# Delta rule on one core: where the first substitution and the projections of the later tiles stand in a hand-written order

## Chip, core and metric

The kernel runs on one core of one Trainium2 chip. The metric is the device time of one execution in microseconds (us). Five engines work side by side and meet through semaphores: PE (matrix multiply), ACT (activation), DVE (vector), POOL (GpSimd) and SP, which here only issues DMA transfers. PEld in the profile is PE's loading of weights.

## The reference, cut to what matters

The network has eight layers over an input of 4 sequences of 1024 tokens with 128 features, each layer of the form `x = x + layer(layernorm(x))`. The change lies in the first, the delta rule, with 8 heads of 16 features:

```python
q = (x @ Wq).reshape(Bb, Ll, H, HD)
k = (x @ Wk).reshape(Bb, Ll, H, HD)
k = k / jnp.maximum(jnp.linalg.norm(k, axis=-1, keepdims=True), 1e-12)
v = jax.nn.silu(x @ Wv).reshape(Bb, Ll, H, HD)
beta = jax.nn.sigmoid(x @ Wb)
...
def step(S, inp):
    qt, kt, vt, bt = inp
    Sk = jnp.einsum('bhk,bhkv->bhv', kt, S)
    S = S + jnp.einsum('bh,bhk,bhv->bhkv', bt, kt, vt - Sk)
    ot = jnp.einsum('bhk,bhkv->bhv', qt, S)
    return (S, ot)
...
return (o - mu) / jnp.sqrt(var + 1e-05) * ln_w + ln_b
```

The seven layers behind it (feed-forward layers, attention, mixtures of experts) are the same in both kernels, and each needs the complete output of the layer ahead of it.

## The kernel before

`l0_attn` (L143) doesn't go token by token. It cuts every sequence into 32 chunks of 32 tokens (C = 32, NS = 32); one chunk of all four sequences fills the 128 partitions. Within a chunk the rule is a triangular system: the Gram matrix of the chunk's keys, scaled by beta, gives a lower triangle L, whose inverse T replaces 32 steps. Between chunks only the 16 x 16 states S are handed on.

**Two sizes of work.** A *tile* is 128 tokens of each sequence, that is four chunks; there are eight. `bring(i)` (L246) normalizes tile i on DVE (xn, four instructions), transposes it on PE (tq) and copies it on ACT into xnT. `gate(i)` (L262) computes beta: matmuls pb, tanh on ACT, one DVE instruction; for some tiles a tiny Silu (hint) goes first, so that ACT loads the table there. `expand(i, j)` (L274) projects half a tile, two chunks, to keys and values: matmuls pp, three ACT instructions (v, vk, sq), a DVE reduction of the squares (rn, L291) and a POOL product. `length(i, n)` (L297) turns rn of n tiles into the inverse norms: a square root on ACT, two DVE instructions.

**For each chunk:** `flip(c)` (L355) scales the keys on POOL, transposes them on PE (tp) and copies them on ACT (kt, bt). `gram(c)` (L372) makes the Gram matrix on PE (wide), copies it on ACT (kk, a ring of two) and sends it in four small transfers to DRAM (ld); after every fourth chunk one transfer brings four matrices back as L, now with one system per partition. `solve(n, part)` (L384) inverts the 128 systems of four chunks on DVE, column by column, 31 columns of two instructions each (L393, L396), cut into eight parts by `PARTS` (L154); after the last part T goes to DRAM (td), and `fetch(c)` (L400) brings it back a chunk at a time as tb. `apply(c)` (L417) multiplies it with keys and values (wp, wu). `attend(c)` (L437) makes the query scores on PE, and DVE masks them (mt, L440). `query(n, g)` (L406) projects the queries (pq). The recurrence itself is up, ux, sp, S, oT, ot, op, o, from L495 on.

**Order.** The scheduler is off in this stage (`manual_schedule`); every engine gets its instructions in the order in which the loop of L490 writes them. It runs over slots -12 to 34. Slot c holds the recurrence of chunk c, `gram(c + 11)`, `fetch(c + 2)`, `apply(c + 1)`, `attend(c + 2)` and `flip(c + 12)`, and one quarter of a substitution: system n is solved in slots 4n - 6 to 4n - 3, two parts a slot, one ahead of the chunk's output (L527) and one at the slot's end, behind the jobs (L556). The jobs of a slot, which are the work on tiles, stand in a table, `jobs` (L305). System 0 needs the Gram matrices of chunks 0 to 3, the last of which is made in slot -8; it is solved in slots -6 to -3. Tiles 4 to 7 are worked on in slots -8 to 0.

**Buffers.** PSUM pools: psc, one buffer (wide); psm, two buffers with tag sm (tq, pb, pp, up, wp, oT, op); ptp, one buffer with tag tp (tp, pq, and pp of tile 7); psp, one buffer for the sum that holds S.

Of the kernel before, what the change touches and what calls it, by code (L numbers as in the profile page):

```python
# [9 lines left out]
F32 = mybir.dt.float32  # L10
# [5 lines left out]
P = 128  # L16
NB, SEQ, D = 4, 1024, 128
TPB = SEQ // P
# [9 lines left out]
class Net:  # L28
# [114 lines left out]
    def l0_attn(self):  # L143
# [8 lines left out]
        H, HD, C = 8, 16, 32  # L152
# [4 lines left out]
        with ExitStack() as c_:  # L157
# [73 lines left out]
            m0 = one.tile([P, TPB, NB, 2], F32, tag="m0", name="m0")  # L231
            r0 = one.tile([P, TPB, NB], F32, tag="r0", name="r0")

            def moments_of(i):

                for b in range(NB):
                    st = two.tile([P, 6], F32, tag="st", name="st", bufs=4)
                    nc.vector.bn_stats(st, x4[:, i, b, :])
                    nc.vector.bn_aggr(m0[:, i, b, :], st)
# [6 lines left out]
            def bring(i):  # L246

                xn = two.tile([P, NB, D], F32, tag="xn", name="xn")
                tp = psm.tile([P, NB, P], F32, tag="sm", name="tq")
                for b in range(NB):  # L250
                    nc.vector.tensor_scalar(
                        xn[:, b, :], x4[:, i, b, :], m0[:, i, b, 0:1], r0[:, i, b : b + 1], ALU.subtract, ALU.mult
                    )
                    nc.tensor.transpose(tp[:, b, :], xn[:, b, :], self.ident)
                nc.scalar.copy(
                    tok[:, 4 * i : 4 * i + 4].rearrange("p c (b t) -> p b c t", b=NB),
                    tp.rearrange("p b (c t) -> p b c t", c=4),
                )
# [3 lines left out]
            def gate(i):  # L262


                if i in (0, 1, 2, 4):
                    nc.scalar.activation(hint, self.eps, AF.Silu)
                pb = psm.tile([P, 4, H], F32, tag="sm", name="pb")
                for j in range(4):
                    mm(pb[:, j, :], lhsT=tok[:, 4 * i + j], rhs=wkvb[:, 256:264], start=True, stop=True)
                bs = beta[:, 4 * i : 4 * i + 4, :]  # L270
                nc.scalar.activation(bs, pb, AF.Tanh, scale=0.5)
                nc.vector.tensor_scalar(bs, bs, 0.5, 0.5, ALU.mult, ALU.add)

            def expand(i, j):  # L274

                c2 = slice(4 * i + 2 * j, 4 * i + 2 * j + 2)
                sh = [P, 2, H, HD]
                pool, tag = (ptp, "tp") if i == TPB - 1 else (psm, "sm")
                pp = pool.tile([P, 2, 256], F32, tag=tag, name="pp")
                for a in range(2):  # L280
                    mm(pp[:, a, :], lhsT=tok[:, 4 * i + 2 * j + a], rhs=wkvb[:, 0:256], start=True, stop=True)
                v = two.tile([P, 2, D], F32, tag="v", name="v")
                nc.scalar.activation(v, pp[:, :, 128:256], AF.Silu)
                pk = pp[:, :, 0:128].rearrange("p c (h d) -> p c h d", h=H)
                nc.scalar.copy(vk[:, c2, :, 0:HD], pk)
                sq = two.tile(sh, F32, tag="sq", name="sq")
                if i == 1:
                    nc.gpsimd.tensor_mul(sq, vk[:, c2, :, 0:HD], vk[:, c2, :, 0:HD])
                else:
                    nc.scalar.square(sq, pk)  # L290
                nc.vector.tensor_reduce(rn[:, c2, :], sq, axis=AX.X, op=ALU.add)  # L291
                nc.gpsimd.tensor_mul(
                    vk[:, c2, :, HD:], v.rearrange("p c (h d) -> p c h d", h=H),
                    beta[:, c2, :].unsqueeze(3).to_broadcast(sh),
                )

            def length(i, n):  # L297
# [9 lines left out]
                -11: [(gate, 1), (expand, 1, 0), (moments_of, 6), (moments_of, 7), (begin, 0)],  # L307
                -10: [(expand, 1, 1), (begin, 1)],
                -9: [(length, 1, 1), (roots_of, 4, 4), (masks,)],
                -8: [(bring, 3), (bring, 4), (gate, 2), (expand, 2, 0), (zeros, 0)],  # L310
                -7: [(expand, 2, 1), (bring, 5), (gate, 3), (expand, 3, 0), (zeros, 1)],
                -6: [(expand, 3, 1), (length, 2, 2), (bring, 6), (zeros, 2)],
                -5: [(bring, 7), (gate, 4), (expand, 4, 0), (zeros, 3)],
                -4: [(expand, 4, 1), (gate, 5), (expand, 5, 0)],
                -3: [(expand, 5, 1), (gate, 6), (expand, 6, 0)],
                -2: [(expand, 6, 1), (gate, 7)],
                -1: [(expand, 7, 0)],
                0: [(expand, 7, 1), (length, 4, 4)],
            }
            moments_of(0)  # L320
            roots_of(0, 1)
# [33 lines left out]
            def flip(c):  # L355

                kn = kns[c % len(kns)]
                nc.gpsimd.tensor_mul(kn[:, :, 0:HD], vk[:, c, :, 0:HD], spread(rn[:, c, :]))
                nc.gpsimd.tensor_mul(vk[:, c, :, 0:HD], kn[:, :, 0:HD], spread(beta[:, c, :]))
                tp = ptp.tile([P, 2, 2, P], F32, tag="tp", name="tp")  # L360
                for i, t in enumerate((kn, vk[:, c])):
                    for g in range(2):
                        nc.tensor.transpose(
                            tp[:, i, g, :], t[:, 4 * g : 4 * g + 4, :].rearrange("p a b -> p (a b)"), self.ident
                        )
                kt = two.tile([P, 2, P], F32, tag="kt", name="kt", bufs=LAG + 3)
                nc.scalar.copy(kt, tp[:, 0])
                bt = two.tile([P, 2, P], F32, tag="bt", name="bt", bufs=3)
                nc.scalar.copy(bt, tp[:, 1])
                kT[c] = (kt, bt)  # L370
# [35 lines left out]
            def query(n, g):  # L406

                if g == 0:
                    qs[n] = two.tile([P, 4, 2, P], F32, tag="qp", name="qp")
                pq = ptp.tile([P, 2, 2, P], F32, tag="tp", name="pq").rearrange("p a b c -> p (a b c)")  # L410
                mm(
                    pq, lhsT=wqp[:, 4 * g : 4 * g + 4, :].rearrange("p a b -> p (a b)"),
                    rhs=tok[:, 4 * n : 4 * n + 4], start=True, stop=True,
                )
                nc.scalar.copy(qs[n][:, :, g, :], pq.rearrange("p (c t) -> p c t", c=4))

            def apply(c):  # L417

                tb = tbs[c % len(tbs)]
                wp = psm.tile([P, 2, P], F32, tag="sm", name="wp")  # L420
                for g in range(2):
                    for j in range(4):
                        mm(
                            wp[32 * j : 32 * j + 32, g, :], lhsT=vk[:, c, 4 * g + j, :], rhs=tb[:, 2 * j + g, :],
                            start=True, stop=True,
                        )
                wu = two.tile([P, 2, P], F32, tag="wu", name="wu")
                nc.scalar.copy(wu, wp)
                return wu
# [60 lines left out]
            for slot in range(-LAG - 1, NS + 3):  # L490
                c, part = slot, (slot + 6) % 4
                n = (slot + 6) // 4
                cut = (2 * part, 2 * part + 1) if 0 <= n < NS // 4 else ()
                if 0 <= c < NS:
                    mt = late.pop(c)  # L495
                    up = psm.tile([P, 2, 64], F32, tag="sm", name="up")
# [30 lines left out]
                for i in cut[0:1]:  # L527
                    solve(n, i)
                if 0 <= c < NS:
                    oT = psm.tile([P, 2, P], F32, tag="sm", name="oT")  # L530
                    for g in range(2):
                        for j in range(4):
                            mm(
                                oT[32 * j : 32 * j + 32, g, :], lhsT=u[:, 4 * g + j, :], rhs=mt[:, 2 * j + g, :],
                                start=True, stop=True,
                            )
                    ot = two.tile([P, 2, P], F32, tag="ot", name="ot")
                    nc.scalar.copy(ot, oT)
                if 0 <= c + 2 < NS:
                    late[c + 2] = attend(c + 2)  # L540
                if 0 <= c < NS:
                    op = psm.tile([P, 2, 64], F32, tag="sm", name="op")
# [10 lines left out]
                    flip(c + LAG + 1)  # L553
                for job, *args in jobs.get(slot, ()):
                    job(*args)
                for i in cut[1:]:  # L556
                    solve(n, i)
                if slot in reloads:
# [1177 lines left out]
```

## Time and profile before

| what | value |
|---|---|
| three timed runs | 2819.35, 2822.51, 2824.38 us (median 2822.51) |
| the profiled execution | 2822.76 us |
| its span, first to last instruction | 2821.0 us |
| delta-rule stage, start to last copy of o (L550) | 0 to 370.2 us |
| DVE busy in the span | 1829.0 us (65%) |
| PE busy in the span | 2554.4 us (91%) |
| start of the mask multiply mt (L440) in slots -2, 0, 2, 4, 8, 12 | 103.5, 116.9, 139.2, 154.6, 186.2, 216.1 us |

Times in the profile count from the start of the span. A row of the timeline gives start, duration, engine, line, operation, what is written and read, and in square brackets how long the engine was idle ahead of it and what ended that idle time. A chain of waits is given by the page too, but its detail begins only after the delta-rule stage; there the stage has to be read from the timeline and the table of stages. PE works each float32 matmul in two passes, so eight matmuls appear as 16.

### The profile page before, as it was taken

How to read it: one execution, taken by the hardware profiler on the slowest of the kernel's cores; microseconds unless marked ns; L12 is line 12 of the kernel's file. 1: busy time of each engine (PE TensorE's matmuls, PEld its weight loads, DVE VectorE, ACT ScalarE, POOL GpSimd, SP SyncE). 2: the span in 40 equal slices, each digit the busy share in tenths (PEclk: the TensorE clock that was granted, in tenths of full speed). 3: DMA queues.
4: the chain of work that ended last, by engine and by line, in shares of the span. 5: the costliest groups of instructions: out<-in, count | busy, mean ns of one | idle time of the engine just before them, and what ended most of it. 6: DMA issues, size and time to landing. Idle time of an engine off the chain costs nothing.

```text
span 2821.0 us, 51973 instructions
## 1 busy us (share of the span) xinstructions
PE 2554.4 (91%) x20384; PEld 1288.8 (46%) x20384; DVE 1829.0 (65%) x3838; ACT 1549.5 (55%) x3520; POOL 172.1 (6%) x286
## 2 busy tenths in 40 slices
PE   5687768999998959999999768999999999999967
PEld 4455536699985533333333343333333333333356
DVE  4788867566663666677676146767776777777234
ACT  4565466655553450665666660666666666666642
POOL 3212000000000000000000050000000000000001
PEclk7899869899998975999999865999999999999968
DMA  2233320000000000010110000000000000000000
GB/s 54 57 74 70 74 64 1 1 2 2 1 2 1 1 1 16 10 16 13 16 18 10 5 1 8 8 8 11 9 9 9 8 12 8 10 8 8 3 9 24
DMA packets 116485, 46.62 MB, mean 17 GB/s; under 512 B 88419, under 2 KB 110860, under 8 KB 116237
## 3 DMA queue, kind: packets, MB, share of 16 engines
q1 hardware_dynamic: 116236, 43.25, 7.7%
q8 instruction: 163, 2.67, 0.4%
q14 instruction: 86, 0.70, 0.1%
HBM read 16.95 MB, written 12.98 MB: 11 GB/s over the span
## 4 chain that ended last, share of the span: by engine, by line
PE 63%; DVE 3%; ACT 2%; POOL 1%; issue 1%; DMA 0%; SPq 0%; POOLq 0%; DVEq 0%; ACTq 0%
PE pb L1261 30%; PE po L1283 15%; PE pa L1236 6%; PE ep L1053 2%; PE tp L119 2%; PE pp L1176 1%; PE gp L1001 1%; PE bp L1066 1%; DVE st L81 1%; ACT xn L108 1%; PE pv L1157 1%; PE op L695 1%; PE bp L1064 0%; DVE mv L82 0%; PE op L694 0%
## 5 line engine op out<-in xcount | busy, mean ns | idle before, releaser
L1265 ACT ACTIVATE es<-pb 128x512 f32<-128x512 f32 x1536 | 836.0, 594 | 561.5 <-PE pb L1261 406.8
L1261 PE MATMUL pb<-q,k 32*128 32x512 f32 x3072 | 957.7, 642 | 0.7 <-ACT es L1265 0.7
L1236 PE MATMUL pa<-k,q 32*128 32x512 f32 x3072 | 912.8, 680 | 16.9 <-DMA q<-q 16.0
L1248 DVE TENSOR_REDUCE bm<-pa 128x2 f32<-128x1024 f32 x512 | 625.9, 1225 | 275.6 <-PE pb L1261 169.7
L1283 PE MATMUL po<-es,v 128*32 128x256 f32 (+1 forms) x5760 | 480.0, 405 | 0.0
L1261 PEld LDWEIGHTS pb<-q,k 32*128 32x128 f32 x3072 | 314.9, 184 | 347.4 <-ACT es L1265 188.9
L1244 DVE TENSOR_REDUCE bm<-pa 128x16 f32<-128x1024 f32 x256 | 312.6, 1222 | 107.4 <-PE pb L1261 60.7
L1283 PEld LDWEIGHTS po<-es,v 128*32 128x32 f32 x5760 | 114.2, 108 | 543.1 <-issue 510.5
L1236 PEld LDWEIGHTS pa<-k,q 32*128 32x128 f32 x3072 | 253.6, 193 | 94.3 <-DVE bm L1248 50.5
L119 PE MATMUL tp<-ident,xn 128*128 128x128 f32 x192 | 65.5, 440 | 56.9 <-ACT xn L108 51.0
L1290 DVE COPY oT<-po 128x512 f32<-128x512 f32 x48 | 32.7, 682 | 109.1 <-PE po L1283 109.1
L393 DVE TENSOR_TENSOR pr<-T,L 128x31 f32<-128x31 f32 (+15 forms) x248 | 95.3, 384 | 7.1
L396 DVE TENSOR_TENSOR T<-T,pr 128x31 f32<-128x31 f32 (+15 forms) x248 | 91.3, 368 | 8.5
L108 ACT ACTIVATE xn<-x,nm,rs 128x128 f32<-128x128 f32 x224 | 89.3, 481 | 7.7 <-DVE nm L105 7.7
L119 PEld LDWEIGHTS tp<-ident,xn 128*128 128x128 f32 x192 | 34.4, 186 | 88.4 <-ACT xn L108 73.2
L1062 DVE SCALAR_TENSOR_TENSOR x<-ep,g,x 128x128 f32<-128x128 f32 x160 | 55.0, 349 | 29.7 <-ACT sc L1060 20.0
L807 ACT ACTIVATE w<-tr,half 128x128 f32<-128x128 f32 x128 | 47.0, 367 | 48.0 <-PE tr L805 45.1
L782 ACT ACTIVATE a<-hp,wb 128x128 f32<-128x128 f32 x128 | 47.1, 368 | 40.8 <-PE hp L778 39.8
L1053 PE MATMUL ep<-L_ffn_expert_w,xnT 128*128 128x512 f32 x128 | 67.9, 620 | 0.0
L513 PE MATMUL sp<-ux,kn 128*128 128x256 f32 x128 | 48.2, 512 | 20.1 <-ACT ux L502 20.1
L1535 POOL MEMSET c<- 128x512 f32 (+1 forms) x2 | 2.3, 1164 | 1021.9 <-PE tp L119 1021.9
L81 DVE BATCH_NORM_STATS2 st<-x 128x6 f32<-128x128 f32 x224 | 57.2, 265 | 9.6 <-PE op L545 4.0
(451 smaller groups left out, 3572.3 us busy)
## 6 DMA issues: line engine op xcount, KB each, us to landing
ld<-kk SPq DMA_DIRECT2D x128, 32.0 KB
L<-ld SPq DMA_DIRECT2D x8, 512.0 KB
td<-T SPq DMA_DIRECT2D x8, 512.0 KB
tb<-td SPq DMA_DIRECT2D x128, 32.0 KB
md<-nt SPq DMA_DIRECT2D x192, 2.0 KB
q<-md SPq DMA_DIRECT2D x192, 2.0 KB
od<-o SPq DMA_DIRECT2D x32, 64.0 KB
on<-od SPq DMA_DIRECT2D x8, 256.0 KB
```

The source lines that it names most:

```text
L81: nc.vector.bn_stats(st, src[:, i, :])
L108: nc.scalar.activation(dst[:, i, :], src[:, i, :], AF.Identity, bias=nm[:, i : i + 1], scale=rs[:, i : i + 1])
L119: nc.tensor.transpose(tp[:, i, :], xn[:, 4 * q + i, :], self.ident)
L393: nc.vector.tensor_mul(pv, T[:, 0 : j + 1, j : j + 1].to_broadcast(sh), L[:, j : j + 1, j + 1 :].to_broadcast(sh))
L396: nc.vector.tensor_sub(T[:, 0 : j + 1, j + 1 :], T[:, 0 : j + 1, j + 1 :], pv)
L1053: nc.tensor.matmul(ep.rearrange("p a b -> p (a b)"), lhsT=self.tok(t), rhs=ew[:, 4 * h : 4 * h + 4, :].rearrange("p a b -> p (a b)"), star ...
L1236: nc.tensor.matmul(pa[:, j % 2, :], lhsT=st["q"][r, i * P : (i + 1) * P], rhs=st["k"][r, n * 512 : (n + 1) * 512], start=True, stop=True,)
L1244: nc.vector.tensor_reduce(out[:, :, 1:9], pa.rearrange("p j (c s) -> p j c s", c=8), axis=AX.X, op=ALU.max)
L1248: nc.vector.tensor_reduce(out[:, :, n : n + 1], pa, axis=AX.X, op=ALU.max)
L1261: nc.tensor.matmul(pb, lhsT=st["k"][r, kc * P : (kc + 1) * P], rhs=st["q"][r, n * 512 : (n + 1) * 512], start=True, stop=True,)
L1265: nc.scalar.activation(es[turn][:, j, :], pb, AF.Exp, scale=scale)
L1283: nc.tensor.matmul(po[r, cols], lhsT=vring[b % 2][:, kc, 4 * g + j, :], rhs=es[:, j, cols], start=kc == 0, stop=True, skip_group_check=True,)
```

## The change

Three things change, all in `l0_attn`.

1. Substitution 0 is taken out of slots -6 to -3 (`0 < n` in `cut`) and put at the end of the jobs of slots -8 (parts 0 and 1), -7 (parts 2 to 4) and -6 (parts 5 to 7). Substitution 1 and the others stay in their slots.
2. Tiles 4 to 7 are worked on later and a piece at a time: tile 4 in slots -5 to -2, tile 5 in slots -3 to 0, tile 6 in slots 4 to 7, tile 7 in slots 8 to 10. `length`, formerly once for tiles 4 to 7, comes in two calls, in slots 1 and 11. The table hint comes for tile 6 as well.
3. Projections of tiles 5 to 7 (tq, pb, pp) take their PSUM buffer from ptp, those of tiles 0 to 4 from psm (`bank`). Tags are renamed to ps in both pools.

```diff
+            def bank(i):
+                return ptp if i > 4 else psm
...
-                tp = psm.tile([P, NB, P], F32, tag="sm", name="tq")
+                tp = bank(i).tile([P, NB, P], F32, tag="ps", name="tq")
...
-                if i in (0, 1, 2, 4):
+                if i in (0, 1, 2, 4, 6):
                     nc.scalar.activation(hint, self.eps, AF.Silu)
-                pb = psm.tile([P, 4, H], F32, tag="sm", name="pb")
+                pb = bank(i).tile([P, 4, H], F32, tag="ps", name="pb")
...
-                pool, tag = (ptp, "tp") if i == TPB - 1 else (psm, "sm")
-                pp = pool.tile([P, 2, 256], F32, tag=tag, name="pp")
+                pp = bank(i).tile([P, 2, 256], F32, tag="ps", name="pp")
...
-                -8: [(bring, 3), (bring, 4), (gate, 2), (expand, 2, 0), (zeros, 0)],
-                -7: [(expand, 2, 1), (bring, 5), (gate, 3), (expand, 3, 0), (zeros, 1)],
-                -6: [(expand, 3, 1), (length, 2, 2), (bring, 6), (zeros, 2)],
-                -5: [(bring, 7), (gate, 4), (expand, 4, 0), (zeros, 3)],
-                -4: [(expand, 4, 1), (gate, 5), (expand, 5, 0)],
-                -3: [(expand, 5, 1), (gate, 6), (expand, 6, 0)],
-                -2: [(expand, 6, 1), (gate, 7)],
-                -1: [(expand, 7, 0)],
-                0: [(expand, 7, 1), (length, 4, 4)],
+                -8: [(bring, 3), (gate, 2), (expand, 2, 0), (zeros, 0)],
+                -7: [(expand, 2, 1), (gate, 3), (expand, 3, 0), (zeros, 1)],
+                -6: [(expand, 3, 1), (length, 2, 2), (zeros, 2)],
+                -5: [(bring, 4), (zeros, 3)],
+                -4: [(gate, 4)],
+                -3: [(expand, 4, 0), (bring, 5)],
+                -2: [(expand, 4, 1)],
+                -1: [(gate, 5), (expand, 5, 0)],
+                0: [(expand, 5, 1)],
+                1: [(length, 4, 2)],
+                4: [(bring, 6)],
+                5: [(gate, 6)],
+                6: [(expand, 6, 0)],
+                7: [(expand, 6, 1)],
+                8: [(bring, 7)],
+                9: [(gate, 7), (expand, 7, 0)],
+                10: [(expand, 7, 1)],
+                11: [(length, 6, 2)],
...
-                cut = (2 * part, 2 * part + 1) if 0 <= n < NS // 4 else ()
+                cut = (2 * part, 2 * part + 1) if 0 < n < NS // 4 else ()
...
                 for job, *args in jobs.get(slot, ()):
                     job(*args)
+                for i in {-8: (0, 1), -7: (2, 3, 4), -6: (5, 6, 7)}.get(slot, ()):
+                    solve(0, i)
                 for i in cut[1:]:
                     solve(n, i)
```

More of the change, by code (lines that the diff above doesn't have):

```diff
@@ L359, in flip @@
                 nc.gpsimd.tensor_mul(vk[:, c, :, 0:HD], kn[:, :, 0:HD], spread(beta[:, c, :]))
-                tp = ptp.tile([P, 2, 2, P], F32, tag="tp", name="tp")
+                tp = ptp.tile([P, 2, 2, P], F32, tag="ps", name="tp")
                 for i, t in enumerate((kn, vk[:, c])):
@@ L409, in query @@
                     qs[n] = two.tile([P, 4, 2, P], F32, tag="qp", name="qp")
-                pq = ptp.tile([P, 2, 2, P], F32, tag="tp", name="pq").rearrange("p a b c -> p (a b c)")
+                pq = ptp.tile([P, 2, 2, P], F32, tag="ps", name="pq").rearrange("p a b c -> p (a b c)")
                 mm(
@@ L419, in apply @@
                 tb = tbs[c % len(tbs)]
-                wp = psm.tile([P, 2, P], F32, tag="sm", name="wp")
+                wp = psm.tile([P, 2, P], F32, tag="ps", name="wp")
                 for g in range(2):
@@ L492, in l0_attn @@
                 n = (slot + 6) // 4
-                cut = (2 * part, 2 * part + 1) if 0 <= n < NS // 4 else ()
+                cut = (2 * part, 2 * part + 1) if 0 < n < NS // 4 else ()
                 if 0 <= c < NS:
                     mt = late.pop(c)
-                    up = psm.tile([P, 2, 64], F32, tag="sm", name="up")
+                    up = psm.tile([P, 2, 64], F32, tag="ps", name="up")
                     for g in range(2):
@@ L529, in l0_attn @@
                 if 0 <= c < NS:
-                    oT = psm.tile([P, 2, P], F32, tag="sm", name="oT")
+                    oT = psm.tile([P, 2, P], F32, tag="ps", name="oT")
                     for g in range(2):
@@ L541, in l0_attn @@
                 if 0 <= c < NS:
-                    op = psm.tile([P, 2, 64], F32, tag="sm", name="op")
+                    op = psm.tile([P, 2, 64], F32, tag="ps", name="op")
                     for g in range(2):
```

## Prediction

> **What bounds the kernel now.** I read the page first: the span is 2821.0 us in a profiled execution of 2822.76 us (median of the three timed runs 2822.51). Everything from about 376 us on (attention, feed-forward layers) is untouched by the change, and each later layer needs the output of the delta rule, so what the delta-rule stage gains or loses goes straight to the end. Then the table of stages (busy time of each engine in chosen stretches):
>
> ```profile
> 40.00:61.00 21.00, 16.26 (x80) 12.38 (x80) 5.46 (x20) 10.01 (x25) 4.57 (x9) 0.50 0.15 38
> 61.00:99.00 38.00, 24.82 (x172) 18.03 (x172) 28.35 (x81) 20.10 (x48) 11.44 (x21) 0.87 0.13 29
> 139.00:264.00 125.00, 103.65 (x1744) 73.36 (x1744) 108.34 (x266) 81.07 (x249) 17.49 (x34) 0.93 0.35 78
> ```
>
> The columns are us, then PE, PEld, DVE, ACT and POOL busy. From 40 to 61 us DVE works 5.5 of 21 us; between 139 and 264 us (slots 2 to 17) it works 108 of 125 us, more than ACT's 81. There DVE is the engine that sets the pace, with PE waiting for it in turn. The timeline shows when the first substitution (solve 0, L393/L396) runs, and what follows it on DVE:
>
> ```profile
> 44.39 0.34 SPq L382 DMA_DIRECT2D L<-ld  x1
> ...
> 60.67 0.42 DVE L291 TENSOR_REDUCE rn<-sq 128x16 f32<-128x256 f32 x1 [2.52 <-ACT sq L290]
> ...
> 61.01 0.18 DVE L393 TENSOR_TENSOR pr<-T,L 128x31 f32<-128x31 f32 x1
> ...
> 99.04 0.21 DVE L396 TENSOR_TENSOR T<-T,pr 128x31 f32<-128x31 f32 x1
> 99.16 0.38 DVE L393 TENSOR_TENSOR pr<-T,L 128x31 f32<-128x31 f32 x1
> 99.33 0.34 SPq L398 DMA_DIRECT2D td<-T  x1
> ```
>
> Its input was asked for at 44.39, but it starts at 61.01, ends at 99.25, and solve 1 follows with no gap. Third, the same timeline at slot 0, the one slot in full swing that in the old kernel still has projection work (expand 7,1 and length):
>
> ```profile
> 116.90 1.23 DVE L440 TENSOR_TENSOR mt<-wide,upper 128x1024 f32<-128x1024 f32 x1 [0.81 <-PE wide L352]
> ...
> 118.73 0.38 ACT L369 COPY bt<-tp 128x256 f32<-128x256 f32 x1
> ...
> 119.17 1.13 PE L281 MATMUL pp<-wkvb,xnT 128*128 128x256 f32 x4 [0.74 <-ACT bt L369]
> ...
> 120.92 0.40 ACT L290 ACTIVATE sq<-pp 128x256 f32<-128x256 f32 x1
> ...
> 121.36 0.42 DVE L291 TENSOR_REDUCE rn<-sq 128x16 f32<-128x256 f32 x1 [3.24 <-ACT sq L290]
> ...
> 122.98 0.39 DVE L300 TENSOR_SCALAR rn<-rn 128x128 f32<-128x128 f32 x1 [1.20 <-ACT rn L299]
> ```
>
> DVE stands idle for 3.24 us until ACT has squared what PE projected, which waited for the single ptp buffer until bt was copied; then 1.20 us for the square root. The substitution's second piece stands behind these on DVE. From this mask multiply (mt, L440, one a slot) to the next are 13.2 us; in slots 8, 12 and 16, which do the same pieces without jobs, 7.1, 7.8 and 8.5.
>
> **What the skill says.** "PSUM — Partial Sum Buffer", Engine vs sequencer instructions: the queues of ScalarE, VectorE and GpSimdE are strict first in, first out. The 3.24 us above is that rule at work. "ScalarE activation tables: per-element evaluation and per-set limits", What a function is on this engine: functions of different sets lie one table load of 1283 ns apart; the trace has 1.28 us. "TensorE: Matmul & The Clock Gate", What's actually happening: the clock halves after idling; the trace agrees in direction: behind a 2.35 us wait in slot 4 the four sp matmuls take 1.72 us against 1.13 in slot 5, pq 1.92 against 1.02.
>
> **Part 1, solve 0 moved to slots -8, -7, -6.** Nothing is added; 62 DVE instructions move. In slot -8 they follow the norm reduction of tile 2 (before at 48.86 to 49.28; without tile 4's four transposes, 0.9 us on PE, and its 0.58 us copy ahead of it I take 48.5). L is 512 KB; the nearest row, the 256 KB reload of od, was issued at 373.62 and used at 376.58, so I bound L's landing by 3 and 4 us: 47.4 to 48.4, just in time. All solves are busy 95.3 + 91.3 us, 23.3 each, 23.8 with issue gaps. Between the pieces stand three reductions (0.42), a beta (0.17), length (0.75) and about 0.8 us of waits: 3.0. End: 48.5 + 23.8 + 3.0 = 75.3, instead of 99.25. The td transfer goes with it: on SP it now stands ahead of gram 6's four ld transfers, which wait until 75.8; kk has two buffers, so this would stop gram 8's copy, due at 83. No cost. The wait of fetch 0 for td (99.33 to 102.20) goes.
>
> What is late next: bring 4 (slot -5) stands behind solve 0 on DVE, and PE's transposes behind that, so PE goes on at 75.3, as before at 74.2 (bring 7). Its transposes (1.15) end at 76.9, gram 7's copy begins at 78.3 (before 80.5), L for solve 1 is issued at 82.6 and here by 86.6. In slots -4 and -3 PE and ACT run one chain through ptp (query, its copy, flip, two copies, pp, v, vk, sq, then DVE's xn, transposes, copy), which at the old durations ends DVE's part at 89.7 and attend 0's matmuls at 93.0 (before 95.4). DVE then does solve 1's first piece, 4.9 us as at 99.2 to 103.5 with gaps: the first mt comes at 94.7 instead of 103.5. Gain 8.8 us. Bounds: 6, if each chain step costs a quarter microsecond more, to 10.5, where attend 0 is the limit.
>
> Slots -2 to 2 took 35.7 us between mt's. Expand 5,1 in slot 0 waits as expand 7,1 did (3.3 us); length is now in slot 1, where ACT's table load and root come behind bt (1.25 us of waiting, 0.75 busy); gate 5 and expand 5,0 in slot -1 wait 1.1 beyond PE's lead. I walk 38.2 us. So mt of slot 2: 133.0 against 139.2, gain 6.2.
>
> **Part 2, tiles 6 and 7 in slots 4 to 11.** The work itself is moved from slots -6 to 0, but the slots it lands in are DVE's. From attend's last matmul (W) the timeline of slot 0 gives: bt copied W+2.35, pp W+3.5, sq W+4.6. mt starts at W+0.1 in slots 4, 5, 8, 9, and 1.5 to 2.9 us later in slots 6, 7, 10, 11, where PE leads. Against the old intervals:
> - Slots 4 and 8 (bring): four xn, 1.1 us on DVE, but PE's next slot waits for xn, ptp and transposes, and ACT copies xnT before ux; ux starts at W+4.0 instead of 2.3. +1.7 each.
> - Slot 5 (gate 6): ptp free W+2.35, table load 1.28, hint 0.2, tanh 0.2: beta at W+4.1, DVE idle since W+1.25. +3.05.
> - Slot 6 (expand 6,0): DVE is by now 3.5 us behind PE, so no wait, 0.4 busy. Slot 7 (expand 6,1): half hidden, +0.35.
> - Slot 9 (gate 7 and expand 7,0 in one ptp buffer): beta W+3.6, pp until W+4.75, sq W+5.95, rn done W+6.4. +5.15.
> - Slot 10: +0.4. Slot 11 (length with a table load): +0.5.
> Sum 13.2 us. Bounds: the DVE time is 1.1 + 3.05 + 0.4 + 1.0 + 1.1 + 5.15 + 0.4 + 0.75 = 13.0, of which DVE's idle time before mt (2.41 in slot 4, 2.70 in slot 8, 0.90 in slot 12) could take at most 6; so from 7, to 18 with every wait in full and PE at its cold clock behind it. Two table loads more than before are in the terms of slots 5 and 11. The renamed tags cost nothing: the same pools with the same buffers. POOL's products move too; POOL waited 102.5 us for sp, which covers them; without that cover they would cost 0.6 us each. After slot 11 nothing differs, and DVE does not catch up.
>
> **Sum.** 2822.76 - 6.2 + 13.2 = 2829.8 for the profiled execution; the median stands 0.25 lower: **2829.5**, slower by 7.0.
>
> **The rivals.** (a) Cover holds: the job waits fall into time in which DVE would wait anyway, and solve 1 keeps its start. Then only the gain at the front is left, 6.2 to 8.8, less about 1: 2816. It decides if DVE's waits before beta in slots 5 and 9 are under 1 us. For it: 6 us of idle time before mt; against it: 3.24 us at slot 0, unhidden. (b) A wash: loss at its low bound 7 with gain 6.2, 2823. (c) The start brings nothing: L or gram 7 late, so solve 1 starts near 99 and tiles 4 to 7 cost in full: 2836 to 2838. For it: bring 4 stands behind solve 0, and PE resumes no earlier than before. That the change doesn't do what it says is excluded: in this stage instructions are issued in the order in which the code writes them, and the new order has solve 0 and the jobs where the title puts them.
>
> **How the numbers follow.** Forecast (2828 to 2834, slower) 0.40; (c) 0.13; (b) 0.30; (a) 0.17. About 0.2% (5.6 us) is what a measurement can tell from no change. Faster 0.17, same 0.30, slower 0.53. The forecast's own range with (c) is 2828 to 2839; the whole range takes in (b) and the edge of (a): 2816.5 to 2839.
>
> **What would show it.** Solve 0 from about 48.5 to 75; first mt near 95, mt of slot 2 near 133. DVE waits of about 2.9 us before beta (ACT) in slot 5, and together 4 to 5 in slot 9. The end of the stage (last copy of o, before at 369.9) near 377. I am wrong if solve 0's td leaves after 80, or if slots 4 to 11 take under 70 us from mt to mt (before 61.5 from slot 4 to slot 12; I expect 75).

## The result and the profile after

| | before | after |
|---|---|---|
| median of 15 runs each | 2823.41 us | 2833.45 us (2826.15 to 2839.81) |
| ratio | | 1.0035, 95% interval 1.0025 to 1.0045 |
| profiled execution, its span | 2822.76, 2821.0 us | 2832.23, 2830.5 us |
| end of the delta-rule stage (last copy of o) | 370.1 us | 379.5 us |
| from there to the end of the span | 2450.9 us | 2451.0 us |

The kernel became slower by 10 us, a third of a per cent. In the two profiled executions, which lie 9.5 us apart, all but 0.1 us of it is in the delta-rule stage. The table of stages of after, in the same stretches as before and then from mt of slot 4 to mt of slot 12 (us, PE, PEld, DVE, ACT and POOL busy, granted clock):

```profile
40.00:61.00 21.00, 15.86 (x82) 12.38 (x79) 14.05 (x41) 10.35 (x26) 6.25 (x11) 0.50 0.20 45
61.00:99.00 38.00, 20.87 (x144) 13.12 (x142) 21.71 (x62) 14.58 (x31) 6.80 (x13) 0.61 0.19 45
151.00:226.00 75.00, 61.29 (x912) 43.04 (x912) 58.15 (x148) 48.49 (x144) 11.86 (x22) 0.91 0.30 66
```

DVE's hole at the start is filled: 14.1 us busy from 40 to 61 instead of 5.5. Slots 4 to 12 take 75 us where before they took 61.5:

```profile
154.50:216.00 61.50, 52.52 (x880) 37.32 (x876) 53.97 (x132) 40.36 (x124) 9.04 (x18) 0.92 0.36 79
```

This is before in the same slots. The 13.5 us more are 4.2 us of DVE work (58.15 against 53.97) and 9.3 us more of DVE not working (16.85 against 7.53). The timeline of after shows the first substitution:

```profile
44.67 0.34 SPq L393 DMA_DIRECT2D L<-ld  x1
...
48.43 0.18 DVE L404 TENSOR_TENSOR pr<-T,L 128x31 f32<-128x31 f32 x1
...
76.28 0.21 DVE L407 TENSOR_TENSOR T<-T,pr 128x31 f32<-128x31 f32 x1
76.40 1.11 DVE L254 TENSOR_SCALAR xn<-x,m,r 128x128 f32<-128x128 f32 x4
76.56 0.34 SPq L409 DMA_DIRECT2D td<-T  x1
76.79 1.24 PE L257 MATMUL tq<-ident,xn 128*128 128x128 f32 x4 [10.89 <-DVE xn L254]
79.31 1.01 ACT L387 COPY kk<-wide 128x1024 f32<-128x1024 f32 x1 [0.66 <-PE wide L363]
```

L was asked for at 44.67 and used at 48.43, so it landed within 3.8 us. Solve 0 ends at 76.5, bring 4's xn follow, and PE had been idle for 10.89 us until they came. The same timeline in slots 5 and 9:

```profile
160.06 1.22 DVE L451 TENSOR_TENSOR mt<-wide,upper 128x1024 f32<-128x1024 f32 x1 [0.97 <-PE wide L363]
...
162.29 1.28 ACT L269 ACT_TABLE_LOAD   x1
...
163.91 0.18 DVE L275 TENSOR_SCALAR beta<-beta 128x32 f32<-128x32 f32 x1 [2.63 <-ACT beta L274]
...
195.78 1.23 DVE L451 TENSOR_TENSOR mt<-wide,upper 128x1024 f32<-128x1024 f32 x1 [0.53 <-PE wide L363]
...
199.38 0.18 DVE L275 TENSOR_SCALAR beta<-beta 128x32 f32<-128x32 f32 x1 [2.37 <-ACT beta L274]
...
201.88 0.42 DVE L293 TENSOR_REDUCE rn<-sq 128x16 f32<-128x256 f32 x1 [2.32 <-ACT sq L292]
...
210.63 1.22 DVE L451 TENSOR_TENSOR mt<-wide,upper 128x1024 f32<-128x1024 f32 x1
```

DVE stands 2.63 us ahead of beta in slot 5, and 2.37 and 2.32 us in slot 9. From mt to mt slot 5 takes 11.5 us and slot 9 14.9.

### The profile page after: what moved, and what is told of

It reads as the page before. It is cut to its first block, busy times and chain, and to the rows that moved or that the text cites. A ratio compares the mean times of both kernels' runs of the same rounds, so it can differ in the third digit from the quotient of the medians.

```text
span 2830.5 us, 51976 instructions
## 1 busy us (share of the span) xinstructions
PE 2564.6 (91%) x20384; PEld 1294.4 (46%) x20384; DVE 1831.4 (65%) x3840; ACT 1553.1 (55%) x3524; POOL 173.8 (6%) x286
## 4 chain that ended last, share of the span: by engine, by line
PE 63%; DVE 3%; ACT 2%; POOL 1%; issue 1%; DMA 0%; SPq 0%; POOLq 0%; DVEq 0%; ACTq 0%
PE pb L1274 30%; PE po L1296 15%; PE pa L1249 6%; PE ep L1066 2%; PE tp L119 2%; PE pp L1189 1%; PE gp L1014 1%; PE bp L1079 1%; ACT xn L108 1%; DVE st L81 1%; PE pv L1170 1%; PE op L708 1%; PE bp L1077 0%; DVE mv L82 0%; PE op L707 0%
## 5 line engine op out<-in xcount | busy, mean ns | idle before, releaser
L1303 DVE COPY oT<-po 128x512 f32<-128x512 f32 x48 | 32.7, 682 | 109.1 <-PE po L1296 109.1
```

## The experiments

The table gives the start of mt in slots -2, 2, 4 and 12, the stretches between them (differences of the starts as given) with the granted clock of PE, the end of the stage (all from one profiled execution each), and the ratio to before with its interval.

| kernel | mt -2 | mt 2 | -2 to 2 (clock) | mt 4 | 4 to 12 (clock) | mt 12 | stage end | ratio |
|---|---|---|---|---|---|---|---|---|
| before | 103.5 | 139.2 | 35.7 (0.88) | 154.6 | 61.5 (0.92) | 216.1 | 370.1 | |
| after | 96.1 | 137.4 | 41.3 (0.77) | 151.1 | 75.2 (0.91) | 226.3 | 379.5 | 1.0035 [1.0025, 1.0045] |
| e1 | 109.1 | 145.5 | 36.4 (0.86) | 160.3 | 62.0 (0.92) | 222.3 | 377.0 | 1.0024 [1.0017, 1.0032] |
| e2 | 97.3 | 137.0 | 39.7 (0.79) | 150.7 | 76.7 (0.89) | 227.4 | 380.8 | 1.0041 [1.0028, 1.0054] |
| e3 | 98.1 | 134.3 | 36.2 (0.87) | 149.7 | 72.3 (0.95) | 222.0 | 375.2 | 1.0019 [1.0009, 1.0029] |
| e4 | 95.6 | 132.8 | 37.2 (0.88) | 146.6 | 74.9 (0.89) | 221.5 | 375.3 | 1.0027 [1.0017, 1.0038] |
| e5 | 93.3 | 134.6 | 41.3 (0.74) | 149.3 | 79.7 (0.83) | 229.0 | 385.3 | 1.0025 [1.0012, 1.0038] |
| e6 | 104.2 | 137.7 | 33.5 (0.92) | 151.4 | 61.7 (0.94) | 213.1 | 367.6 | 0.9983 [0.9975, 0.9992] |
| e7 | 95.8 | 133.0 | 37.2 (0.84) | 150.2 | 75.3 (0.86) | 225.5 | 379.5 | 1.0057 [1.0034, 1.0080] |
| e8 | 94.1 | 127.7 | 33.6 (0.80) | 142.0 | 73.0 (0.91) | 215.0 | 369.4 | 0.9994 [0.9984, 1.0005] |
| e9 | 103.7 | 142.6 | 38.9 (0.76) | 157.1 | 69.3 (0.90) | 226.4 | 380.0 | 1.0026 [1.0018, 1.0034] |
| e10 | 104.1 | 139.8 | 35.7 (0.88) | 155.2 | 67.9 (1.00) | 223.1 | 373.6 | 1.0024 [1.0017, 1.0031] |
| e11 | 103.6 | 139.3 | 35.7 (0.88) | 154.6 | 67.9 (0.90) | 222.5 | 376.2 | 1.0040 [1.0024, 1.0056] |
| e12 | 104.8 | 141.2 | 36.4 (0.73) | 156.0 | 62.0 (0.94) | 218.0 | 372.0 | 0.9991 [0.9983, 0.9998] |

How exact is a stretch of one execution? e9, e10 and e11 have before's code up to slot 4. e10 and e11 give 35.7 us for slots -2 to 2, as before did; e9 gives 38.9, at a granted clock of 0.76 instead of 0.88. So a stretch is good to a few tenths at a like clock, and can be off by 3 us at another. The first mt has such a spread too: six kernels with before's code up to it (before, e6, e9 to e12) have it at 103.5 to 104.8, three with after's code up to it (after, e3, e7) at 96.1, 98.1 and 95.8. From the last o to the end the kernels take 2447.6 to 2454.9 us although nothing differs there: totals are therefore judged by the ratios. From mt of slot 12 to the end of the stage before takes 154.0 us and after 153.2, the others 153 to 156; only e10 is shorter, 150.5. So after catches up no more than 0.8 us behind slot 11.

### Each half of the change alone: e1 and e2

e1 is before with only solve 0 moved:

```diff
-                cut = (2 * part, 2 * part + 1) if 0 <= n < NS // 4 else ()
+                cut = (2 * part, 2 * part + 1) if 0 < n < NS // 4 else ()
...
+                for i in {-8: (0, 1), -7: (2, 3, 4), -6: (5, 6, 7)}.get(slot, ()):
+                    solve(0, i)
```

> The kernel before with only substitution 0 moved to slots -8 to -6; the tiles' jobs and buffers stay as before. Theory A (the loss is DVE's waiting for the jobs of tiles 5 to 7 in slots -1 to 11, in front of the substitution's second piece): nothing is lost, the front gain of 6 to 9 us is kept, 2814 to 2818. Theory B (the loss is the single ptp buffer that tiles 5 to 7 now share with flip and query): the same 2814 to 2818. Theory C (moving substitution 0 gains nothing, because the tiles' work is then late behind it): 2822 to 2825.

Measured: ratio 1.0024, the first mt at 109.1, 5.6 us *later* than before, though solve 0 ended at 82.9 instead of 99.3. The timelines of DVE and ACT in before and then in e1 tell why:

```profile
74.16 1.11 DVE L251 TENSOR_SCALAR xn<-x,m,r 128x128 f32<-128x128 f32 x4
...
80.49 1.01 ACT L376 COPY kk<-wide 128x1024 f32<-128x1024 f32 x1 [0.25 <-ACT sq L290]
...
85.22 0.42 DVE L291 TENSOR_REDUCE rn<-sq 128x16 f32<-128x256 f32 x1 [0.83 <-ACT sq L290]
```

```profile
82.76 1.10 DVE L251 TENSOR_SCALAR xn<-x,m,r 128x128 f32<-128x128 f32 x4
...
89.09 1.01 ACT L376 COPY kk<-wide 128x1024 f32<-128x1024 f32 x1 [0.25 <-ACT sq L290]
...
95.61 0.42 DVE L291 TENSOR_REDUCE rn<-sq 128x16 f32<-128x256 f32 x1 [6.31 <-ACT sq L290]
...
101.89 0.42 DVE L291 TENSOR_REDUCE rn<-sq 128x16 f32<-128x256 f32 x1 [3.65 <-ACT sq L290]
...
104.44 0.18 DVE L393 TENSOR_TENSOR pr<-T,L 128x31 f32<-128x31 f32 x1
...
109.06 1.21 DVE L440 TENSOR_TENSOR mt<-wide,upper 128x1024 f32<-128x1024 f32 x1
```

The tiles' xn, beta and rn stand on DVE between and behind the pieces of solve 0. The last xn, of tile 7, come behind all of solve 0, at 82.76 instead of 74.16, and PE's transposes of them, with what stands behind these on PE and ACT, come as much later: gram 7's copy at 89.09 instead of 80.49. DVE has solve 0 behind it by then and waits, 6.31 us for a square for which before it waits 0.83, and then 3.65 us where in before it is still busy with solve 0. (The two waits between 82.76 and 89.09, 2.79 and 2.04 us, are the same in before.) Solve 1 starts at 104.4 instead of 99.2, behind the last of these reductions. Its L had been asked for at 93.43, 11 us earlier, so it stands behind the tiles' chain through PE, ACT and DVE and not behind its own input.

e2 is after with solve 0 left in its old slots (`0 <= n` again, and the loop for solve 0 gone).

> The changed kernel with substitution 0 back in slots -6 to -3: jobs and buffers as changed. A: the loss of the jobs in full (13.7 us from slot 4 to 12, about 3 to 5 in slots -2 to 1), less what an emptier front brings to substitution 0 (about 4 us): 2833 to 2839. B: the same. C: as the changed kernel, 2833.

Measured: ratio 1.0041, within the interval of after. Its first mt, beside that of after, each from the timeline of DVE (e2 first):

```profile
97.34 1.21 DVE L451 TENSOR_TENSOR mt<-wide,upper 128x1024 f32<-128x1024 f32 x1
```

```profile
96.07 1.23 DVE L451 TENSOR_TENSOR mt<-wide,upper 128x1024 f32<-128x1024 f32 x1
```

Of the 7.4 us by which after's first mt is early, 6.2 come without moving solve 0: with most jobs of tiles 4 to 7 gone from slots -8 to -3 even the old solve 0 starts at 57.4 instead of 61.0 and ends at 92.9. The two halves don't add: +0.24% and +0.41% alone, +0.35% together. Solve 0's early place costs 5.6 us at the first mt where the tiles are still there. Where they have left, no gain is shown: the 1.2 us between 97.3 and 96.1 lie inside the spread of after's own code (95.8 to 98.1), and in slot 2 e2 is ahead, 137.0 against 137.4.

### What the job waits on DVE cost: e3

e3 is after with each slot's projections put behind the slot's second substitution piece, from slot -2 on:

```diff
                 for job, *args in jobs.get(slot, ()):
-                    job(*args)
+                    if slot < -2 or job is bring:
+                        job(*args)
...
                 for i in cut[1:]:
                     solve(n, i)
+                for job, *args in jobs.get(slot, ()):
+                    if not (slot < -2 or job is bring):
+                        job(*args)
```

> The changed kernel, but from slot -2 on gate, expand and length are written behind the substitution's second piece instead of ahead of it (bring stays ahead). Only DVE's order changes. A: DVE's waits before beta, rn and length go, some 2.5 us in slot 5, 2 in slot 7, 4.7 in slot 9, and about 3 in slots -1 to 1: 2822 to 2826. B: nothing changes by more than 2 us, 2831 to 2834, as pb and pp still wait for the one ptp buffer.

Measured: ratio 1.0019. Slots -2 to 2 take 5.1 us less (36.2, at a clock of 0.87 instead of 0.77, so that part of it can be the clock). Slots 4 to 12 take 72.3 us: of the 13.7 us that after loses there only 2.9 come back, although the waits before beta are gone. Timeline of e3, DVE:

```profile
193.34 1.22 DVE L451 TENSOR_TENSOR mt<-wide,upper 128x1024 f32<-128x1024 f32 x1 [0.47 <-PE wide L363]
...
197.92 0.17 DVE L275 TENSOR_SCALAR beta<-beta 128x32 f32<-128x32 f32 x1
...
199.15 0.42 DVE L293 TENSOR_REDUCE rn<-sq 128x16 f32<-128x256 f32 x1 [1.06 <-ACT sq L292]
...
204.70 1.22 DVE L451 TENSOR_TENSOR mt<-wide,upper 128x1024 f32<-128x1024 f32 x1
...
212.38 1.22 DVE L451 TENSOR_TENSOR mt<-wide,upper 128x1024 f32<-128x1024 f32 x1
...
221.96 1.23 DVE L451 TENSOR_TENSOR mt<-wide,upper 128x1024 f32<-128x1024 f32 x1 [3.74 <-PE wide L363]
```

Slot 9 shrinks from 14.9 to 11.4 us; but slot 11 grows from 7.8 to 9.6, with DVE waiting 3.74 us for PE's scores. The waits of DVE before mt in slots 5 to 12 sum to 8.0 us, against 2.9 in after and 3.6 in before. Where DVE no longer waits in the middle of a slot, it waits at its end. Slot by slot the result is mixed: slots 5, 6, 9 and 10 together lose 2.4 us to before instead of after's 7.7, but slots 4, 7, 8 and 11 lose 8.4 instead of 6.1. So the waits in mid-slot did cost in the first four, and something else sets the other four. The theory behind the prediction's part 2, that DVE's own sum sets all these slots, falls here.

### One PSUM buffer or two: e4

```diff
             def bank(i):
-                return ptp if i > 4 else psm
+                return psm
```

> The changed kernel with the projections of all tiles in psm (two buffers) instead of ptp (one) for tiles 5 to 7. A: the waits shorten only by the time that pb, pp and tq wait for the copy of bt, 0.6 us a job in slots 4 to 10: 2829 to 2833. B: most of the 10 us comes back, 2823 to 2827.

Measured: ratio 1.0027. Slots 4 to 12 are unchanged (74.9), so the single ptp buffer is not what makes them long. Slots -2 to 2 take 37.2 instead of 41.3. The rows say where (after first, then e4; DVE in slots -1 and 0):

```profile
105.63 1.22 DVE L451 TENSOR_TENSOR mt<-wide,upper 128x1024 f32<-128x1024 f32 x1
107.74 0.18 DVE L275 TENSOR_SCALAR beta<-beta 128x32 f32<-128x32 f32 x1 [0.89 <-ACT beta L274]
110.90 0.42 DVE L293 TENSOR_REDUCE rn<-sq 128x16 f32<-128x256 f32 x1 [2.98 <-ACT sq L292]
...
120.21 0.42 DVE L293 TENSOR_REDUCE rn<-sq 128x16 f32<-128x256 f32 x1 [3.24 <-ACT sq L292]
```

```profile
105.32 1.22 DVE L451 TENSOR_TENSOR mt<-wide,upper 128x1024 f32<-128x1024 f32 x1
106.45 0.17 DVE L275 TENSOR_SCALAR beta<-beta 128x32 f32<-128x32 f32 x1
107.33 0.42 DVE L293 TENSOR_REDUCE rn<-sq 128x16 f32<-128x256 f32 x1 [0.70 <-ACT sq L292]
...
115.63 0.42 DVE L293 TENSOR_REDUCE rn<-sq 128x16 f32<-128x256 f32 x1 [2.24 <-ACT sq L292]
```

With two buffers slot -1 waits 0.70 us in all instead of 3.87, and slot 0 2.24 instead of 3.24: 4.2 us together, which is the 4.1 us that the stretch recovers. The clock in it is also higher (0.88 against 0.77); whether PE's shorter waits raise the clock or the clock shortens the waits is not told apart.

### Bring 4 ahead of solve 0: e5

```diff
-                -8: [(bring, 3), (gate, 2), (expand, 2, 0), (zeros, 0)],
+                -8: [(bring, 3), (bring, 4), (gate, 2), (expand, 2, 0), (zeros, 0)],
...
-                -5: [(bring, 4), (zeros, 3)],
+                -5: [(zeros, 3)],
```

> The changed kernel with one job put back: bring 4 stands in slot -8 again, ahead of substitution 0 on DVE, instead of in slot -5 behind it. A (moving substitution 0 gained nothing at the front because bring 4, and with it PE and gram 7, stand behind it): gram 7's copy comes about 8 us earlier (70 to 73 instead of 79.3), the first mt at 88 to 92 instead of 96.1, total 2825 to 2829. C (the front is set by the chain of DVE work, whatever stands first): first mt at 95 or later, total 2832 to 2834.

Measured: ratio 1.0025, not told apart from after. The front, timeline of ACT and DVE in e5:

```profile
69.77 1.01 ACT L387 COPY kk<-wide 128x1024 f32<-128x1024 f32 x1 [1.40 <-issue]
...
82.17 1.01 ACT L387 COPY kk<-wide 128x1024 f32<-128x1024 f32 x1 [6.38 <-DMA ld<-kk]
...
93.29 1.22 DVE L451 TENSOR_TENSOR mt<-wide,upper 128x1024 f32<-128x1024 f32 x1
```

Gram 7's copy comes at 69.77 instead of 79.31, so bring 4 behind solve 0 was what held it. But the next copy waits 6.38 us for its kk buffer: the ld transfers stand on SP behind td, which waits for solve 0 (it ended at 78.0). The first mt gains 2.8 us of the 9.5. The 79.7 us of its slots 4 to 12 say little: the granted clock there was 0.83, after's 0.91, and the profiled execution took 2838.6 us where the median of its twelve is 2832.2.

### What a microsecond in slots 4 to 11 costs on each engine: e9, e10, e11

Three kernels are before with work added to each of slots 4 to 11, whose result nothing reads: three ACT copies of 128x256 (e9), two matmuls of pp's shape into a ptp tile (e10), or two DVE reductions of 128x256 (e11).

```diff
                 for job, *args in jobs.get(slot, ()):
                     job(*args)
+                if 4 <= slot < 12:
+                    extra()
```

> The kernel before with ACT work alone added where jobs stand, in slots 4 to 11: three copies of 128x256 on scratch data (about 1.15 us a slot, what expand costs on ACT); nobody waits for them but what follows on ACT. From mt of slot 4 to mt of slot 12 before: 61.5 us. A (in these slots DVE alone sets the pace): 61.5 to 63.5. D (the recurrence's chain through PE and ACT is as near the limit as DVE, so that a job costs on every engine it touches): 66 to 70.

> The kernel before with PE work alone added where jobs stand, in slots 4 to 11: two matmuls of 128x256 into the ptp buffer (what expand costs on PE, 1.1 us a slot, and the wait for the copy of bt, 0.6 us), read by nobody. A: 61.5 to 63.5 us from mt of slot 4 to mt of slot 12. D: 65 to 70.

> The kernel before with DVE work alone added where jobs stand, in slots 4 to 11: two reductions of 128x256 on scratch data (0.84 us a slot), without any wait. A: 61.5 + 6.7 less the idle time of at most 3.6 us in slots 8 and 12: 65 to 68 us from mt of slot 4 to mt of slot 12. D: 64 to 67, as slots that PE and ACT limit hide it.

Measured in slots 4 to 12, against 61.5 us: e9 +7.8 for 8.8 us more of ACT being busy (49.13 against 40.36), e10 +6.4 for 9.0 us of added matmuls and the buffer they hold (at a clock of 1.00 against before's 0.92, which may flatter it; what the buffer adds is not told apart), e11 +6.4 for 6.2 us more of DVE being busy (60.20 against 53.97). The table of stages for that stretch, of e9 and of e11:

```profile
157.10:226.40 69.30, 54.34 (x880) 37.65 (x872) 54.15 (x133) 49.13 (x148) 8.87 (x18) 0.90 0.32 70
```

```profile
154.60:222.50 67.90, 54.13 (x880) 37.60 (x872) 60.20 (x149) 40.35 (x124) 9.26 (x18) 0.90 0.34 72
```

In e9 DVE's work is before's (54.15 against 53.97), yet the stretch is longer by 7.8 us: all of it is DVE waiting, as here in the timeline of e9:

```profile
182.45 1.21 DVE L449 TENSOR_TENSOR mt<-wide,upper 128x1024 f32<-128x1024 f32 x1
...
191.78 1.22 DVE L449 TENSOR_TENSOR mt<-wide,upper 128x1024 f32<-128x1024 f32 x1 [4.58 <-PE wide L361]
```

ACT is busy 40 of 61.5 us before the change, PE 52.5 and DVE 54. None is free all the same: over the eight slots added work is paid nearly in full on ACT (7.8 of 8.8 us) and in full on DVE (6.4 for 6.2), and for the larger part on PE (6.4 for 9.0). Where it is paid differs. Time from mt to mt, in us:

| slots | before | e9 (ACT) | e10 (PE) | e11 (DVE) | after |
|---|---|---|---|---|---|
| 5, 6, 9, 10 together | 34.00 | 34.15 | 33.90 | 37.07 | 41.66 |
| 4, 7, 8, 11 together | 27.48 | 35.09 | 33.98 | 30.79 | 33.54 |

In slots 5, 6, 9 and 10 the added work on ACT or PE lengthens next to nothing (0.15 us at most), while DVE's is paid: DVE sets these slots. The whole of the 7.6 and 6.5 us is paid in slots 4, 7, 8 and 11, where DVE then waits for PE's scores. The clock doesn't make this pattern: before, e1, e6 and e12 have the same code in slots 4 to 11, and their slots 5, 6, 9 and 10 agree within 0.2 us (33.8 to 34.0), the other four within 0.7 (27.5 to 28.2). The loop goes round PE and ACT (up, ux, sp, S, query, scores) into DVE's mt, and in these four slots that round sets the time. Two limits of the test: e9's copies stand on ACT just ahead of ux, so that sp waits 1.49 us for ux instead of 0.31 in before (slot 5), and another place on ACT was not tried; and work was added to all eight slots at once, so it is not shown that work in slots 5, 6, 9 and 10 alone would cost nothing.

### Placing the jobs where PE leads, and all remedies at once: e7 and e8

e7 is e3 with the jobs of tiles 6 and 7 in other slots:

```diff
-                1: [(length, 4, 2)],
-                4: [(bring, 6)],
-                5: [(gate, 6)],
-                6: [(expand, 6, 0)],
-                7: [(expand, 6, 1)],
-                8: [(bring, 7)],
+                1: [(length, 4, 2), (bring, 6)],
+                2: [(gate, 6), (expand, 6, 0)],
+                5: [(expand, 6, 1)],
+                6: [(bring, 7)],
                 9: [(gate, 7), (expand, 7, 0)],
-                10: [(expand, 7, 1)],
-                11: [(length, 6, 2)],
+                10: [(expand, 7, 1), (length, 6, 2)],
```

> As the run with gate, expand and length behind the second piece, and the jobs of tiles 6 and 7 only in slots 1, 2, 5, 6, 9 and 10, where PE and ACT are ahead of DVE. D (there, the jobs' work on PE and ACT lengthened the recurrence's chain in slots 4, 6, 7, 8 and 11, where PE is not ahead): mt of slot 4 to mt of slot 12 takes 64 to 68 us instead of 72.3, total 2822 to 2826. A alone (only DVE's own work and waits count): 70 to 73 us, total as that run, 2827 to 2830.

Measured: 75.3 us for slots 4 to 12, no gain over after, though three jobs had left them. Slots 4, 7, 8 and 11 come down from 33.5 to 30.7 us, but slots 5, 6, 9 and 10, where the jobs now stand, grow from 41.7 to 44.6 (at a clock of 0.86 against 0.91). The six runs lie in two groups (2829.3 and 2832.2; 2841.1 to 2848.1 us), and the profile is of the first; why, stays open.

e8 is e7 with e4's buffers and a front in which tiles 4 and 5 are done by slot -2 and slots -1 and 0 have no jobs:

```diff
+                -8: [(bring, 3), (bring, 4), (gate, 2), (expand, 2, 0), (zeros, 0)],
...
+                -5: [(gate, 4), (expand, 4, 0), (zeros, 3)],
+                -4: [(bring, 5), (expand, 4, 1)],
+                -3: [(gate, 5), (expand, 5, 0)],
+                -2: [(expand, 5, 1)],
```

> All that the runs so far point to: substitution 0 early, bring 4 ahead of it, tiles 4 and 5 a slot earlier, gate, expand and length behind the second piece, tiles 6 and 7 in slots where PE leads, all projections in the pool with two buffers. If front gain and late costs add as read so far: first mt 88 to 91, mt of slot 4 to 12 in 64 to 67 us, total 2808 to 2816, faster than both kernels. If the front is bound otherwise: 2820 to 2826.

Measured: ratio 0.9994, the time of before. Its mt of slot 4 is 12.6 us earlier than before's, the largest front gain of all; slots 4 to 12 give back 11.5 of it (73.0 against 61.5). What this kernel took out of the start and put into slots 4 to 11 is paid there again, nearly to the microsecond.

### Leaving the tiles where they were, behind the second piece: e6 and e12

e6 is before with slot 0's expand and length put behind the substitution's second piece (e3's edit, from slot 0 on).

> The kernel before; in slot 0 alone, expand 7,1 and length are written behind the substitution's second piece, so that DVE no longer waits ahead of it (3.24 and 1.20 us in the profile of before). A (such a wait on DVE costs what it lasts): the interval from mt of slot 0 to mt of slot 1 falls from 13.2 to 9 us, total 2818 to 2820. D (the chain of PE and ACT, which still does the jobs ahead of up and ux, takes the place of the wait): 10.5 to 12 us, total 2820 to 2822.

Measured: ratio 0.9983, faster than before. Timeline of e6, DVE in slot 0:

```profile
117.71 1.23 DVE L440 TENSOR_TENSOR mt<-wide,upper 128x1024 f32<-128x1024 f32 x1 [0.80 <-PE wide L352]
...
122.18 0.42 DVE L291 TENSOR_REDUCE rn<-sq 128x16 f32<-128x256 f32 x1 [0.71 <-ACT sq L290]
...
123.80 0.39 DVE L300 TENSOR_SCALAR rn<-rn 128x128 f32<-128x128 f32 x1 [1.20 <-ACT rn L299]
...
128.65 1.23 DVE L440 TENSOR_TENSOR mt<-wide,upper 128x1024 f32<-128x1024 f32 x1 [0.29 <-PE wide L352]
```

The wait of 3.24 us before rn becomes 0.71, and slot 0 takes 10.9 us instead of 13.2, both at a granted clock of 1.00. The number is in D's range, but the reason is not D's: of the 2.5 us of waiting that went, 2.3 came off the slot, as A says, and DVE waits only 0.29 us at its end. A's 9 us were missed because the 1.20 us for the root stayed. The stage ends 2.5 us earlier; the ratio, about 4.8 us, is more than this, and where the rest lies is not shown.

e12 is before with tile 7's last two halves and length one slot earlier, nothing in slot 0, and slot -1's jobs behind the second piece:

```diff
-                -2: [(expand, 6, 1), (gate, 7)],
-                -1: [(expand, 7, 0)],
-                0: [(expand, 7, 1), (length, 4, 4)],
+                -2: [(expand, 6, 1), (gate, 7), (expand, 7, 0)],
+                -1: [(expand, 7, 1), (length, 4, 4)],
```

> The kernel before, with the last jobs of tile 7 one slot earlier (expand 7,0 in slot -2, expand 7,1 and length in slot -1) and in slot -1 behind the substitution's second piece: the opposite direction of the change, no job left in slots 0 and later. A and D agree: mt of slot 0 to mt of slot 1 falls from 13.2 to 7 to 9 us, slots -2 to 0 lengthen by at most 2: 2817 to 2820 against 2823 before, faster than both kernels.

Measured: ratio 0.9991. Slot 0 falls to 7.1 us as meant, but slot -1 grows from 6.0 to 12.0. Timeline of e12, DVE:

```profile
113.09 1.22 DVE L439 TENSOR_TENSOR mt<-wide,upper 128x1024 f32<-128x1024 f32 x1
...
116.52 0.40 DVE L291 TENSOR_REDUCE rn<-sq 128x16 f32<-128x256 f32 x1
...
125.08 1.22 DVE L439 TENSOR_TENSOR mt<-wide,upper 128x1024 f32<-128x1024 f32 x1 [4.53 <-PE wide L351]
```

The wait before rn is gone, and 4.53 us of waiting for PE's scores stand before mt. Part of this is the clock: granted in slot -1 were 0.52 in e12 and 1.00 in before, and e9, with before's code there and a clock of 0.59, takes 9.2 us for the slot and waits 2.75 before mt. That leaves an estimated 12.0 - 9.2 = 2.8 us for the jobs' PE and ACT parts. The profiled execution is also the slowest of the 21 (2828.46 us, median 2820.77), so this page is not the typical one.

## Why the prediction was right, and where its reasons were not

**The total.** Forecast +7.0 us, measured +10 (+9.5 between the two profiled executions), slower as forecast and inside the range. The stage ended (start of the last copy of o) at 379.2, forecast near 377. In the terms of the sum, up to mt of slot 4: 3.5 us gained; slots 4 to 12: 13.7 lost; behind them 0.8 gained; the rest of the network 0.1 lost; together 9.5.

**Part 1, the times.** Solve 0 ran from 48.4 to 76.5 (forecast 48.5 to 75.3), gram 7's copy came at 79.3 (78.3), attend 0's matmuls ended at 95.9 (93.0), the first mt came at 96.1 (94.7). Right within 3 us each.

**Part 1, the step that failed: whose gain it is.** The prediction puts the 8.8 us at the first mt under "solve 0 moved". e2 has 6.2 of the measured 7.4 without that move, and e1, with that move alone, loses 5.6. The gain belongs to the tiles' leaving the start; the early substitution fits into the space that they leave, and no gain of its own is shown. The walk along solve 0 came out because it was done in the new order, with the tiles gone; it was never done with one half of the change alone. DVE's idle time at 40 to 61 us looked like room for a 23 us job, but the instructions between which that job is put are what PE and ACT live on. That is the order rule that the prediction cites from "PSUM — Partial Sum Buffer", Engine vs sequencer instructions, in the other direction: e1's xn, 8.6 us late behind solve 0, and its wait of 6.31 us, 0.83 in before, agree with it.

**Part 1, the term that was mis-sized.** "I walk 38.2 us" for slots -2 to 2; it was 41.3. With the first mt 1.4 us later than forecast, mt of slot 2 gained 1.8 us, not 6.2. The terms named there don't give 38.2 either: slot 0 loses length (1.20 us of waiting and 1.34 of work in before), slot 1 gains 2.0, slot -1 1.1, which is under 1 us more than 35.7; the rest of the walk isn't written down. Slot -1 waits 3.87 us (forecast 1.1) and slot -2, for which nothing was taken, 2.02. With two buffers instead of one (e4) the waits in slots -1 and 0 are 4.2 us shorter, at a higher clock, so the pool of tiles 5 to 7 probably costs here; how much of the 4.2 is the clock stays open.

**Part 2, the numbers.** Forecast 13.2, measured 13.7. By slots, forecast and then measured intervals: slot 4 8.8 and 8.9, slot 5 12.05 and 11.5, slot 9 14.15 and 14.9. The waits were forecast at about 2.9 in slot 5 (2.63) and 4 to 5 in slot 9 (4.69). Slot 11 is 1.5 above its term (7.8 against 6.3), slot 6 1.0 below (7.4 against 8.4).

**Part 2, the mechanism, incomplete.** Summed on DVE the loss comes out (4.2 us of work and 9.3 of waiting), and the prediction took that sum as the cause. e3 removes waits and recovers 2.9 of 13.7; e9 adds 8.8 us of ACT work alone and loses 7.8. So there are two rounds, DVE's and the one of PE and ACT, and which of them sets the time changes from slot to slot: DVE's in slots 5, 6, 9 and 10, the other in 4, 7, 8 and 11. The prediction had read this pattern off the starts of mt (PE leads in slots 6, 7, 10 and 11, where the mt that ends slots 5, 6, 9 and 10 stands), but then called all the slots DVE's. Of the 13.7 us, 7.7 fall into DVE's four slots and 6.1 into the others. The forecast was right in size, it seems, because the prediction's waits of DVE are the PE and ACT work as seen from DVE; this is argued, not tested. What e9 and e11 show is how little room is left over the eight slots together: 8.8 - 7.8 = 1.0 us on ACT, none on DVE. The length of the PE and ACT round itself was not measured. The remedies drawn from it failed too (e7's 75.3 us, e8's 73.0): the slots in which PE leads, for which whole jobs were meant, didn't take them for nothing.

**The rivals.** (a), that cover holds, needed waits under 1 us in slots 5 and 9; they were 2.63 and 4.69. (b), a wash, and (c), a start that brings nothing, lie on either side of the result: the loss was at its likely value, and the gain, 1.8 us at mt of slot 2 and 3.5 at mt of slot 4, between none and the forecast's 6.2. Solve 1 started at 91.7, not near 99, so (c)'s mechanism did not come.

**Still open.** e7's two groups of times, and what sets the granted clock in slots -2 to 2 (0.73 to 0.92 among these kernels), which is worth up to 3 us there.

The lowest ratio found is that of e6, before with expand and length of slot 0 moved behind a substitution piece: 0.9983 (0.9975 to 0.9992); e12's 0.9991 (0.9983 to 0.9998) is not told apart from it. Before with the change's large reorder and every remedy (e8) only comes back to where it started.

## What to carry to other kernels

Idle time on one engine at the start of a pipeline is room for a long job only if nothing that other engines need stands behind that job on the same engine; test a two-part change by halves, for the gain may belong to the other half. In a loop whose engines wait for each other in turn, a split of the lost time into work and waits of one engine always adds up and proves nothing: add a little work to each engine alone, and see in which part of the loop it is paid. Before moving work to another place, try it at the same place behind what can run meanwhile; here that small edit won 0.17%, where the large one lost 0.35%.

## What was not expected of the hardware

The four sp matmuls of a slot take either 1.13 us or 2.08 us in most slots of these kernels, and which it is changes from slot to slot. The timeline of PE in after and in e5, the same slot:

```profile
165.07 1.13 PE L524 MATMUL sp<-ux,kn 128*128 128x256 f32 x4 [0.67 <-ACT ux L513]
```

```profile
162.74 2.08 PE L524 MATMUL sp<-ux,kn 128*128 128x256 f32 x4 [0.67 <-ACT ux L513]
```

The wait just ahead is the same 0.67 us. So it is not that wait alone that decides, as the prediction's reading of 1.72 against 1.13 us behind a 2.35 us wait suggested; around the second row, from 163 to 170 us, the granted clock of e5 was 0.50, in after it was 1.00 from 158 to 172. Two or three such slots more are 1.9 to 2.9 us more of PE time, and the same code can have them or not: in slots 4 to 11 before has two of 2.07 and 2.08 us, and e1, the same code there, none above 1.73.
